# One list of parts per step in a relational graph layer: token values moved to GpSimd, degrees, statistics and normalisation cut into halves

## The chip, the cores and the metric

The kernel runs on one core of one Trainium2 chip. A core has five engines that work side by side, each through its own instructions in order: TensorE (PE, matrix products; its weight loads are shown as PEld), VectorE (DVE), ScalarE (ACT), GpSimd (POOL) and SyncE (SP, which here only issues DMAs). They wait for each other through semaphores. The metric is the device time of the whole program in microseconds (us), lower is better.

## The reference

One layer with a residual, over 64 samples of 256 tokens and 768 features, all in float32. `adj` holds integers 0 and 1 (about 1.6% ones) and is used both as adjacency and as relation index.

```python
h = jnp.maximum(_layernorm(x, axis=-1), 0.0)
adj = heads.astype(hs.dtype); radj = jnp.swapaxes(adj, 1, 2)
deg = adj.sum(-1); rdeg = radj.sum(-1)          # deg_c, rdeg_c: the same, 1 where 0
ctx = jnp.matmul(adj, hs @ Wadj.T + badj) / deg_c[..., None]
ctx = ctx + jnp.matmul(radj, hs @ Wrev.T + brev) / rdeg_c[..., None]
ctx = ctx + hs @ Wself.T + bself
agg = jnp.einsum('bij,bijr->bir', adj, E[rels])
rel = agg @ Wr.T + br * deg[..., None]
ragg = jnp.einsum('bij,bijr->bir', radj, E[rr])
rel = rel + ragg @ Wrr.T + brr * rdeg[..., None]
x = x + ctx + rel
```

## The kernel before

**What is multiplied.** The three 768x768 products of a sample are one product of a left matrix (256 tokens by three blocks: aggregated over `adj`, aggregated over its transpose, and the tokens themselves) with a right matrix (three weight blocks by three thirds of 256 output columns). The tokens are cut into halves a and b, so the left blocks are called a0, a1, a2, b0, b1, b2. Instead of 18 block products the kernel makes 15, each of a sum of left blocks with a sum of weight blocks (table `PRODUCTS`: number, left sum, right sum). GpSimd makes the left sums (`combine_left`, L490); the weight sums are made once.

**Two sweeps.** The weights of 15 products don't fit at once. Sweep 1 makes products 10, 5, 8, 11, 14, 2, 3, 13 for all 64 samples, keeps the left blocks in DRAM (`store_left`) and the partial output; sweep 2 loads both (`load_left`, `load_sums`) and makes products 7, 9, 15, 6, 4, 12, 1.

**Words.** From some sample on (`IN_WORDS`: product 9 or 7 from 1, 5, 15 and 4 from 2, 10 from 3, 11 from 4) a product is made from left and right values that were each split into a rounded part and a rest (`split_left`, `split_right`); its first two passes are `product_first` (L496), written "10a", "5a", "11a" below, and its third is in `product` (L507).

**A step of sweep 1** (`step1(t)`) does three samples at once: the products of M = t; for A = t+1 the aggregation (`aggregate`, six parts u0 to u5: four matmuls into a PSUM bank `pa`, L473, then a DVE product with the row of reciprocal degrees into `X`, L478), the token features (`self_features`, two GpSimd passes over `xT`, L462, then a Relu on ScalarE, L465) and the left sums; for N = t+2 the degrees (ScalarE sums over `adj`), the layer norm's statistics, and the normalised rows `hilo` in two words (ScalarE L424, DVE L430). `pa` has two PSUM banks, so the matmuls of part u(k+2) wait until DVE has read part u(k).

**Token values.** `statistics` (L373) makes mean and variance of N with the DVE's batch-norm instructions (L379, L380), and then a handful of tiny instructions on 2 to 20 numbers a partition: variance plus epsilon (L381), its power -0.5 on GpSimd (L382), the negated mean (L383), degrees clipped to 1 (L390), their reciprocal (L391), and a copy (L393). The tile `cols` then goes through a PE transpose (`pt`, L400), ScalarE (`line`, L402), DRAM (`d`, L405) and a broadcast load (`row`, L407). The next step's aggregation and `self_features` read `row`.

**The order.** The whole program is under manual scheduling: each engine runs its instructions in the order in which the Python code emits them. `ORDER1` and `ORDER2` list the products and, as plain numbers, the aggregation parts; `others_of_step`, `first_step`, `last_step` and `start` hang all other work on positions of that list. In `step1` the statistics of N are emitted at position 1, right behind part u0:

```python
if k == 0:
    degrees(N)
if k == 1:
    statistics(N)
```

A path for inputs with other integers in `adj` (`general_path`) follows and is skipped by a flag.

Of the kernel before, what the change touches and what calls it, by code (L numbers as in the profile page):

```python
# [9 lines left out]
F32 = mybir.dt.float32  # L10
# [7 lines left out]
P = 128  # L18
# [48 lines left out]


ORDER1 = (
    (10, "z", None, None),  # L70
    0,
    (5, "y", None, None),
    1,
    (10, "z", None, ((1, 1, 2),)),
    (5, "y", None, ((1, 1, 0),)),
    2,
    3,
    (8, "y", None, ((1, 1, 2),)),
    4,
    (11, "w", None, None),  # L80
    5,
    (14, "y", 2, ((-1, 0, 2),)),
    (11, "w", None, ((-1, 0, 2),)),
    (2, "z", 0, ((1, 0, 1),)),
    (3, "w", 1, ((1, 1, 2),)),
    (13, "y", 3, ((-1, 0, 0),)),
)
ORDER2 = (
    (7, "v", None, None),
    (9, "x", None, ((1, 0, 0),)),  # L90
    (15, "u", None, None),
    (7, "v", None, ((1, 0, 1, 2),)),
    (6, "x", None, ((1, 0, 1),)),
    (15, "u", None, ((1, 1, 1, 2),)),
    (4, "t", None, None),
    (12, "x", 4, ((-1, 1, 1),)),
    (4, "t", None, ((-1, 0, 1), (1, 1, 1))),
    (9, "x", None, None),
    (1, "x", 5, ((-1, 1, 0),)),
)  # L100
# [14 lines left out]
def kernel(  # L115
# [61 lines left out]
    others = const.tile([P, B], F32, name="others")  # L177
    flag = const.tile([1, 1], I32, name="flag")

    def main_path(main: ExitStack):  # L180
# [178 lines left out]
        def degrees(b):  # L359

            s = S[b]
            t = tok[b % 2]
            s["a"] = first2.tile([P, C, 2, L], F32R, tag="a", name=f"a_{b}")
            s["squares"] = first2.tile([P, C], F32, tag="squares", name=f"squares_{b}")
            for c in range(C):
                for k in range(2):
                    nc.scalar.activation(
                        s["a"][:, c, k, :], s["adj"][:, c, k, :], AF.Copy, accum_out=t[:, c, 4 - k : 5 - k]
                    )
                junk = first1.tile([P, L], BF16, tag="junk", name=f"junk_{b}_{c}")  # L370
                nc.scalar.activation(junk, s["adj"][:, c, 1, :], AF.Square, accum_out=s["squares"][:, c : c + 1])

        def statistics(b):  # L373
            s = S[b]
            t, v = tok[b % 2], cols[b % 2]
            stats = first2.tile([P, C, 2, 6], F32, tag="stats", name=f"stats_{b}")
            for c in range(C):
                for n in range(2):
                    nc.vector.bn_stats(stats[:, c, n, :], (s["o", c] if b == 0 else s["x"][:, c, :])[:, ts(n, HO)])  # L379
                nc.vector.bn_aggr(v[:, c, NMEAN : RSTD + 1], stats[:, c, :, :])  # L380
            nc.vector.tensor_scalar(v[:, :, RSTD], v[:, :, RSTD], EPS, None, op0=ALU.add)  # L381
            nc.gpsimd.tensor_tensor(v[:, :, RSTD], v[:, :, RSTD], half, op=ALU.pow)  # L382
            nc.vector.tensor_scalar(v[:, :, NMEAN], v[:, :, NMEAN], -1.0, None, op0=ALU.mult)  # L383

            rest = first2.tile([P, C], F32, tag="rest", name=f"rest_{b}")
            nc.vector.scalar_tensor_tensor(
                rest, s["squares"], 1.0, t[:, :, 3], op0=ALU.mult, op1=ALU.subtract, accum_out=others[:, b : b + 1]
            )
            nc.vector.tensor_scalar(t[:, :, 0:2], t[:, :, 3:5], 0.0, None, op0=ALU.is_gt)
            nc.vector.tensor_scalar(v[:, :, RDEG : RRDEG + 1], t[:, :, 3:5], 1.0, None, op0=ALU.max)  # L390
            nc.vector.reciprocal(v[:, :, RDEG : RRDEG + 1], v[:, :, RDEG : RRDEG + 1])  # L391
            to = v.rearrange("p c (k r) -> p c k r", k=2)[:, :, :, :NROW]
            nc.vector.tensor_copy(to, t.unsqueeze(2).to_broadcast([P, C, 2, NROW]))  # L393

        def spread(b):

# [518 lines left out]
```

## Time and profile before

| | |
|---|---|
| time, median of 2 runs | 3025.98 us (3023.38 and 3028.57) |
| the profiled execution's own time | 3028.58 us |
| its span, first to last instruction | 3026.8 us |
| mean granted TensorE clock | 0.971 of full |
| TensorE busy | 2797.6 us, 92% |
| VectorE / ScalarE / GpSimd busy | 2002.9 / 1495.4 / 1781.1 us |
| DMA moved | 698.50 MB, 231 GB/s on average |

What lies outside the span is 3028.58 - 3026.8 = 1.8 us. Sweep 1 takes the first two thirds of the span (TensorE's last product of sweep 1 ends at about 1942 us), sweep 2 the rest. A timeline row gives start, length, engine, line, operation, output and inputs, and in square brackets how long the engine stood idle before it and who ended that; when rows are pipelined, a row's length is a little more than the distance to the next. A row that begins with a stretch A:B gives for each engine its busy time there (with the number of instructions), then the granted clock, the share of time that the DMA engines were busy, and GB/s.

### The profile page before, as it was taken

What the parts mean: (1) busy time and instruction counts of PE and PEld (TensorE: products, weight loads), DVE (VectorE), ACT (ScalarE), POOL (GpSimd) and SP (SyncE); (2) the same over time, 40 slices, a digit from 0 to 9 for tenths busy, and PEclk for the clock granted to TensorE, in tenths of its full rate; (3) what the DMA queues carried; (4) which work ended last, traced back from release to release, by engine and by line L of the source; (5) the groups of instructions that cost most, each with busy time, mean ns of one, the idle gap of its engine ahead of it and who ended that gap; (6) DMA issues with size and microseconds to landing.
All of it is one profiled execution on the core that took longest, in us unless ns stands there. A gap on an engine that the chain in (4) does not pass through costs nothing.

```text
span 3026.8 us, 43782 instructions
## 1 busy us (share of the span) xinstructions
PE 2797.6 (92%) x16112; PEld 2516.0 (83%) x16112; DVE 2002.9 (66%) x3340; ACT 1495.4 (49%) x2734; POOL 1781.1 (59%) x905
## 2 busy tenths in 40 slices
PE   4779999999999999999999999799999999999999
PEld 2668888887887788888878888689999999999998
DVE  5466766766766767667667666466666666666665
ACT  3345555555555555555555555244444444444443
POOL 4365666666666656666666666555555555555553
PEclk8899999999999999999999999899999999999999
DMA  8456666666666666666666665667676667767674
GB/s 269 144 204 237 216 241 237 225 241 227 235 232 225 234 232 220 241 236 227 236 229 232 237 223 214 253 218 253 232 251 235 241 244 243 244 235 253 233 251 155
DMA packets 240355, 698.50 MB, mean 231 GB/s; under 512 B 19444, under 2 KB 100852, under 8 KB 223752
## 3 DMA queue, kind: packets, MB, share of 16 engines
q1 hardware_dynamic: 203272, 393.64, 39.5%
q10 hardware_dynamic: 36864, 302.01, 25.7%
q8 instruction: 129, 2.11, 0.3%
q14 instruction: 90, 0.74, 0.1%
HBM read 439.46 MB, written 256.11 MB: 230 GB/s over the span
## 4 chain that ended last, share of the span: by engine, by line
PE 58%; DVE 8%; issue 0%; DMA 0%; ACT 0%; POOL 0%; ACTq 0%; DVEq 0%; POOLq 0%
PE x L507 18%; PE y L507 9%; PE pa L473 4%; PE w L507 4%; PE u L496 3%; PE v L496 3%; PE t L496 3%; PE x L496 3%; PE z L507 3%; DVE cols L381 3%; DVE stats L379 2%; PE z L496 2%; PE u L507 2%; PE t L507 2%; PE w L496 2%; PE v L507 2%
## 5 line engine op out<-in xcount | busy, mean ns | idle before, releaser
L490 POOL TENSOR_TENSOR X<-X,Xs 128x768 f32<-128x768 f32 x256 | 473.3, 1861 | 497.4 <-DVE l L271 273.4
L473 PE MATMUL pa<-a,hilo 128*128 128x512 f32 x1536 | 437.8, 408 | 168.7 <-DVE X L478 144.9
L507 PE MATMUL y<-w,X 128*128 128x256 f32 x2304 | 578.8, 405 | 10.1 <-DVE o L520 6.4
L507 PEld LDWEIGHTS y<-w,X 128*128 128x128 f32 x2304 | 468.2, 205 | 88.4 <-issue 7.5
L473 PEld LDWEIGHTS pa<-a,hilo 128*128 128x128 f32 x1536 | 266.4, 192 | 238.2 <-DVE X L478 172.4
L462 POOL TENSOR_TENSOR xT<-xT,row 128x1536 f32<-128x1536 f32 (+1 forms) x128 | 447.7, 3498 | 16.3 <-DMA row<-d 11.3
L255 ACT ACTIVATE top<-l 128x768 f32<-128x768 f32 x350 | 285.4, 815 | 283.6 <-DVE l L272 174.0
L478 DVE TENSOR_TENSOR X<-pa,row 128x512 f32<-128x512 f32 x384 | 258.8, 687 | 186.6 <-PE pa L473 186.6
L507 PE MATMUL x<-w,X 128*128 128x256 f32 x1548 | 357.4, 381 | 7.9 <-DVE o L520 6.5
L272 DVE SCALAR_TENSOR_TENSOR l<-l,top 128x768 fp32r<-128x768 f32 x350 | 333.9, 954 | 12.1
L490 POOL TENSOR_TENSOR b2-a<-Xs,X 128x768 f32<-128x768 f32 x64 | 116.6, 1821 | 373.2 <-DVE X L478 373.2
L507 PEld LDWEIGHTS x<-w,X 128*128 128x128 f32 x1548 | 286.5, 191 | 42.5 <-issue 6.9
L490 POOL TENSOR_TENSOR a1+b<-X 128x768 f32<-128x768 f32 x64 | 117.1, 1829 | 268.2 <-PE w L507 246.6
L430 DVE SCALAR_TENSOR_TENSOR hilo<-x,cols,top_h 128x768 fp32r<-128x768 f32 x128 | 129.8, 1014 | 107.2 <-ACT top_h L255 107.1
L271 DVE TENSOR_TENSOR l<-X,top 128x768 fp32r<-128x768 f32 x186 | 176.8, 950 | 16.5 <-POOL X L490 16.5
L507 PE MATMUL w<-w,a1+b 128*128 128x256 f32 x768 | 178.6, 383 | 5.2 <-DVE o L522 5.2
L507 PE MATMUL x<-w,Xs 128*128 128x256 f32 x768 | 176.1, 379 | 0.0
L507 PE MATMUL z<-w,Xs 128*128 128x256 f32 x768 | 176.1, 379 | 0.0
L520 DVE TENSOR_TENSOR o<-o,x 128x256 f32<-128x256 f32 x128 | 53.9, 421 | 167.8 <-PE x L507 167.8
L507 PEld LDWEIGHTS w<-w,a1+b 128*128 128x128 f32 x768 | 143.2, 192 | 24.4 <-DVE o L522 5.8
L402 ACT ACTIVATE line<-pt 128x128 f32<-128x128 f32 x64 | 17.7, 277 | 293.4 <-PE pt L400 293.4
L465 ACT ACTIVATE Xs<-xT 128x1536 f32<-128x1536 f32 x64 | 95.0, 1484 | 127.2 <-POOL xT L462 123.2
(183 smaller groups left out, 5882.1 us busy)
## 6 DMA issues: line engine op xcount, KB each, us to landing
kept_X<-X ACTq DMA_DIRECT2D x64, 1536.0 KB
X<-kept_X ACTq DMA_DIRECT2D x64, 1536.0 KB
o<-in_x_dram SPq DMA_DIRECT2D x128, 384.0 KB
xT<-in_x_t_dram SPq DMA_DIRECT2D x64, 768.0 KB
kept_Xs<-Xs ACTq DMA_DIRECT2D x64, 768.0 KB
sums<-o SPq DMA_DIRECT2D x128, 384.0 KB
Xs<-kept_Xs ACTq DMA_DIRECT2D x64, 768.0 KB
o<-sums SPq DMA_DIRECT2D x128, 384.0 KB
```

Of the source, the lines that this page charges most:

```text
L255: nc.scalar.activation(top.rearrange("p (f i) -> p f i", i=of.shape[-1]), of, AF.Copy)
L271: nc.vector.tensor_tensor(others, value, top, op=ALU.subtract)
L272: nc.vector.scalar_tensor_tensor(diff, others.bitcast(F32), -STEP, top, op0=ALU.mult, op1=ALU.add)
L381: nc.vector.tensor_scalar(v[:, :, RSTD], v[:, :, RSTD], EPS, None, op0=ALU.add)
L430: nc.vector.scalar_tensor_tensor(hilo[:, 1, c, :], S[b]["x"][:, c, :], rstd, top, op0=ALU.mult, op1=ALU.subtract)
L462: eng.tensor_tensor(v, v, row[:, k : k + 1, :].to_broadcast([P, f1 - f0, L]), op=op)
L465: nc.scalar.activation(S[b]["Xs"], xT, AF.Relu)
L473: nc.tensor.matmul(pa, hilo[:, part, c, ts(f, P)], s["a"][:, c, :, :].rearrange("p s i -> p (s i)"), start=(k == 0), stop=(k == 2 * C - 1),)
L478: nc.vector.tensor_mul(s["X"][:, f, :, :].rearrange("p s i -> p (s i)"), pa, s["row"][:, 2:4, :].rearrange("p s i -> p (s i)"))
L490: (eng or nc.gpsimd).tensor_tensor(L[name], L[x], L[y], op=op)
L496: nc.tensor.matmul(bank, l[k][:, f, :], r[k][:, f, :], start=(k == 0 and f == 0), stop=(k == 1 and f == F - 1))
L507: nc.tensor.matmul(bank, l[:, f, :], r[:, f, :], start=(start and f == 0), stop=(row is None and f == F - 1), skip_group_check=not start,)
```

## The change

The two order tables and the functions around them are replaced by six strings. Each names the parts of a step in the order in which they are emitted; a mark ' behind a name means one sample later, '' two later. `FIRST` and `SECOND` are the first two steps with the start, `STEP1` a step of sweep 1, `LAST1` its last, `FIRST2` and `STEP2` sweep 2. `run` reads such a string and calls the functions. With it:

- `statistics`, `degrees`, `normalise` and `self_features` take a half (a token half, or one of the two passes), so that the halves are parts of their own at places of their own.
- The tiny instructions of `statistics` become `token_values`, a part of its own, and run on GpSimd, except the reciprocal, which stays on DVE. `others` has one number per token half and sample instead of one per sample.
- The products keep their operands. Their order in a step changes: 10a, 5a, 5, 10, 8, 11a, 11, 14, 3, 2, 13 with the aggregation in the order u1 u2 u0 u3 u4 u5; in sweep 2 the products' order stays.

```diff
-ORDER1 = (
-    (10, "z", None, None),
-    0,
-    (5, "y", None, None),
-    1,
...
+STEP1 = """
+left' degrees0'' u1' self0' 10a u2' 5a statistics0'' self1' u0' 5 statistics1'' 10 s11 degrees1'' adj''' o1' u3' relu' 8 11a u4' tokens'' u5' a0+a1+b0+b1 xt'' 11 normalise1'' b2-a1' spread'' store' second1'' a2+b2 14 b0+b1' s10' 3 normalise0'' second0'' a1+b1' 2 13 x''' out0 a1+b0+b1' out1 o0' s5'
+"""
...
+STEP2 = """
+7a a0+a2+b0+b2 a1+a2' b1+b2' a0+a2' 9 s4 15a 7 6 load'' s9' 15 4a tokT 12 s7' o0' 4 out0 s15' 9a' a0+a2+b2' 1 out1 o1'
+"""
...
-        def statistics(b):
+        def statistics(b, c):
+            s = S[b]
+            if c == 0:
+                s["stats"] = first2.tile([P, C, 2, 6], F32, tag="stats", name=f"stats_{b}")
+            for n in range(2):
+                nc.vector.bn_stats(s["stats"][:, c, n, :], (s["o", c] if b == 0 else s["x"][:, c, :])[:, ts(n, HO)])
+            nc.vector.bn_aggr(cols[b % 2][:, c, NMEAN : RSTD + 1], s["stats"][:, c, :, :])
+
+        def token_values(b):
+
             s = S[b]
             t, v = tok[b % 2], cols[b % 2]
...
-            nc.vector.tensor_scalar(v[:, :, RSTD], v[:, :, RSTD], EPS, None, op0=ALU.add)
+            nc.gpsimd.tensor_scalar(v[:, :, RSTD], v[:, :, RSTD], EPS, None, op0=ALU.add)
             nc.gpsimd.tensor_tensor(v[:, :, RSTD], v[:, :, RSTD], half, op=ALU.pow)
-            nc.vector.tensor_scalar(v[:, :, NMEAN], v[:, :, NMEAN], -1.0, None, op0=ALU.mult)
-
-            rest = first2.tile([P, C], F32, tag="rest", name=f"rest_{b}")
-            nc.vector.scalar_tensor_tensor(
-                rest, s["squares"], 1.0, t[:, :, 3], op0=ALU.mult, op1=ALU.subtract, accum_out=others[:, b : b + 1]
-            )
-            nc.vector.tensor_scalar(t[:, :, 0:2], t[:, :, 3:5], 0.0, None, op0=ALU.is_gt)
-            nc.vector.tensor_scalar(v[:, :, RDEG : RRDEG + 1], t[:, :, 3:5], 1.0, None, op0=ALU.max)
+            nc.gpsimd.tensor_scalar(v[:, :, NMEAN], v[:, :, NMEAN], -1.0, None, op0=ALU.mult)
+
+            nc.gpsimd.tensor_tensor(others[:, b, :], s["squares"], t[:, :, 3], op=ALU.subtract)
+            nc.gpsimd.tensor_scalar(t[:, :, 0:2], t[:, :, 3:5], 0.0, None, op0=ALU.is_gt)
+            nc.gpsimd.tensor_scalar(v[:, :, RDEG : RRDEG + 1], t[:, :, 3:5], 1.0, None, op0=ALU.max)
             nc.vector.reciprocal(v[:, :, RDEG : RRDEG + 1], v[:, :, RDEG : RRDEG + 1])
             to = v.rearrange("p c (k r) -> p c k r", k=2)[:, :, :, :NROW]
-            nc.vector.tensor_copy(to, t.unsqueeze(2).to_broadcast([P, C, 2, NROW]))
+            nc.gpsimd.tensor_copy(to, t.unsqueeze(2).to_broadcast([P, C, 2, NROW]))
...
-        def self_features(b, parts=((0, F),)):
+        def self_features(b, k):
...
+        def run(order, M, sweep, parts, places):
+
+            for item in order.split():
+                name = item.rstrip("'")
+                b = M + len(item) - len(name)
+                stem, digit = name[:-1], name[-1]
...
+                elif name in parts:
+                    part = parts[name]
+                    multiply(b, *part, sweep)
+                    if part[-1] and part[0] in IN_WORDS and b == IN_WORDS[part[0]] - 1:
+                        split_right(places, part[0])
+                elif name in of_sample:
+                    of_sample[name](b)
+                elif stem in of_part:
+                    of_part[stem](b, int(digit))
...
         for t in range(B):
-            step1(t)
+            order = FIRST if t == 0 else SECOND if t == 1 else STEP1 if t + 1 < B else LAST1
+            run(order, t, 1, PARTS1, PLACES1)
```

How the rows stand on VectorE in a steady step of sweep 1. In the names the first number after `pa` is the aggregation part, for `o` the token half, and after `X`, `y`, `z`, `l_11` the sample; the last is a running number; `waits` lists the semaphores. Before, products of sample 20:

```order
L478 TENSOR_TENSOR X_21_5030<-pa_0_5044,row_4898 128x512 [waits DMAHW7_49,DMAHW2_49,PE_49]
L380 BN_AGGR cols_104<-stats_5050 128x2 [waits DVE_49]
L381 TENSOR_SCALAR cols_104<-cols_104 128x2 [waits DVE_49]
L383 TENSOR_SCALAR cols_104<-cols_104 128x2
L386 SCALAR_TENSOR_TENSOR rest_5060,others<-squares_5035,tok_102 128x2 [waits Activation_49]
L389 TENSOR_SCALAR tok_102<-tok_102 128x2x2
L390 TENSOR_SCALAR cols_104<-tok_102 128x2x2
L391 RECIPROCAL cols_104<-cols_104 128x2x2 [waits DVE_49]
L393 COPY cols_104<-tok_102 128x4x5
L478 TENSOR_TENSOR X_21_5030<-pa_1_5080,row_4898 128x512 [waits PE_49]
```

The same engine after, products of sample 21:

```order
L401 BN_AGGR cols_105<-stats_5281 128x2 [waits DVE_49]
L543 TENSOR_TENSOR o_1_21_5083<-o_1_21_5083,z_21_5247 128x256 [waits PE_49]
L293 TENSOR_TENSOR l_11_21_5310<-X_21_4992,top_21_5313 128x768 [waits Activation_49]
L294 SCALAR_TENSOR_TENSOR l_11_21_5311<-l_11_21_5310,top_21_5313 128x768 [waits DVE_49]
L501 TENSOR_TENSOR X_22_5232<-pa_3_5325,row_5153 128x512 [waits PE_49]
L543 TENSOR_TENSOR o_1_21_5083<-o_1_21_5083,y_21_5267 128x256 [waits PE_49]
L501 TENSOR_TENSOR X_22_5232<-pa_4_5353,row_5153 128x512 [waits PE_49]
L414 RECIPROCAL cols_105<-cols_105 128x2x2 [waits Pool_49]
L501 TENSOR_TENSOR X_22_5232<-pa_5_5367,row_5153 128x512 [waits PE_49]
L545 TENSOR_TENSOR o_0_21_5222<-o_0_21_5222,w_21_5339 128x256 [waits DMAHW6_49,DMAHW4_49,PE_49]
```

Between the statistics and part u1 stood six tiny instructions; now only the reciprocal is left, and it stands between parts u4 and u5 and waits for GpSimd.

GpSimd in the same place, before:

```order
L490 TENSOR_TENSOR a1+b_20_5010<-X_20_4789 128x768 [waits PE_49]
L490 TENSOR_TENSOR X_20_4789<-a1+b_20_5010,X_20_4789 128x6x128 [waits DMAHW4_49,Pool_49]
L462 TENSOR_TENSOR xT<-xT,row_4898 128x1536 [waits DMAHW7_49,DMAHW2_49]
L462 TENSOR_TENSOR xT<-xT,row_4898 128x1536 [waits Pool_49]
L382 TENSOR_TENSOR cols_104<-cols_104,half 128x2 [waits DVE_49]
L490 TENSOR_TENSOR X_20_4789<-X_20_4789 128x6x128
```

and after:

```order
L513 TENSOR_TENSOR a1+b_21_5198<-X_21_4992 128x768 [waits PE_49]
L513 TENSOR_TENSOR X_21_4992<-a1+b_21_5198,X_21_4992 128x6x128 [waits DMAHW6_49,Pool_49]
L485 TENSOR_TENSOR xT<-xT,row_5153 128x1536 [waits DMAHW4_49,DMAHW0_49]
L485 TENSOR_TENSOR xT<-xT,row_5153 128x1536 [waits Pool_49]
L407 TENSOR_SCALAR cols_105<-cols_105 128x2 [waits DVE_49]
L408 TENSOR_TENSOR cols_105<-cols_105,half 128x2 [waits Pool_49]
L409 TENSOR_SCALAR cols_105<-cols_105 128x2
L411 TENSOR_TENSOR others<-squares_5235,tok_103 128x2 [waits Activation_49]
L412 TENSOR_SCALAR tok_103<-tok_103 128x2x2
L413 TENSOR_SCALAR cols_105<-tok_103 128x2x2
L416 COPY cols_105<-tok_103 128x4x5 [waits Pool_49]
L513 TENSOR_TENSOR X_21_4992<-X_21_4992 128x6x128
```

Six tiny instructions have joined the power behind the two passes over `xT`, ahead of the sum a0+a1+b0+b1 (last row) that product 14 reads. The copy (L416) doesn't wait for DVE's reciprocal.

More of the change, by code (lines that the diff above doesn't have):

```diff
@@ L357, in store_sums, with degrees @@
             nc.sync.dma_start(to[:, c, :], s["o", c])
-        def degrees(b):
+        def degrees(b, c):
             s = S[b]
             t = tok[b % 2]
[L363 to L371, printed above, removed]
```

333 lines of the change are left out of this document (111 added, 222 removed).

## The prediction

> **What bounds the kernel now.** I read the page's busy times first, then busy times by stretch, since two sweeps with a start and a seam can't be read from one average.
>
> ```profile
> span 3026.8 us, 43782 instructions
> PE 2797.6 (92%) x16112; PEld 2516.0 (83%) x16112; DVE 2002.9 (66%) x3340; ACT 1495.4 (49%) x2734; POOL 1781.1 (59%) x905
> ```
> ```profile
> 0.00:215.20 215.20, 139.77 (x552) 111.94 (x553) 116.21 (x190) 81.54 (x155) 98.13 (x53) 0.85 0.59 205
> 215.20:1880.40 1665.20, 1535.92 (x8296) 1351.15 (x8295) 1146.78 (x2092) 892.62 (x1742) 1073.59 (x523) 0.98 0.65 231
> 1880.40:2000.00 119.60, 100.61 (x507) 89.05 (x506) 65.01 (x78) 37.30 (x47) 62.49 (x30) 0.89 0.64 230
> 2000.00:3000.00 1000.00, 1000.00 (x6628) 944.16 (x6628) 664.26 (x965) 479.18 (x783) 546.84 (x301) 1.00 0.69 240
> ```
>
> The first number behind each length is PE. Sweep 2 (fourth row) has PE busy for 1000.00 of 1000 us at full clock: no order can gain there. What can be gained lies in the start (75 us idle), in steady sweep 1 (1665.20 - 1535.92 = 129 us idle, and a clock of 0.98), and in the seam (19 us). Steady sweep 1 is 58 steps, between the ends of product 13 of steps 3 and 61; the last row ends step 62.
>
> ```profile
> 214.90 0.47 PE L512 MATMUL y<-rows,tokT 128*128 128x256 f32 x1
> ...
> 1880.13 0.47 PE L512 MATMUL y<-rows,tokT 128*128 128x256 f32 x1
> ...
> 1905.51 0.47 PE L512 MATMUL y<-rows,tokT 128*128 128x256 f32 x1
> ```
>
> (1880.13 - 214.90) / 58 = 28.71 us a step. Step 62 has no sample N, so no statistics and no token values, but all products and all six aggregation parts: 1905.51 - 1880.13 = 25.38 us. The PE work of a step thus fits in 25.4 us plus one transpose, and 3.3 us a step are something else. The list of PE's waits and the timeline of one step name it:
>
> ```profile
> PE pa L473 <- DVE X L478: 144.9, 62, 7.0
> ```
> ```profile
> 1026.35 1.08 PE L473 MATMUL pa<-a,hilo 128*128 128x512 f32 x4
> 1029.65 1.19 PE L473 MATMUL pa<-a,hilo 128*128 128x512 f32 x4 [2.22 <-DVE X L478]
> 1030.68 2.75 PE L507 MATMUL y<-w,X 128*128 128x256 f32 x12
> ...
> 1057.65 1.27 PE L473 MATMUL pa<-a,hilo 128*128 128x512 f32 x4 [2.22 <-DVE X L478]
> 1058.71 4.42 PE L507 MATMUL y<-w,X 128*128 128x256 f32 x12
> ```
>
> Once a step PE stands 2.22 us, 62 times, for a bank that DVE hasn't read. Behind every second gap (this one, not the one before) twelve matmuls take 4.42 instead of 2.75 us: the clock has dropped. That is 1.67 us in two steps, 0.8 a step. 25.4 + 2.2 + 0.8 = 28.4 of the 28.7. Why is DVE late? Its timeline there, and GpSimd's:
>
> ```profile
> 1025.78 2.66 DVE L381 TENSOR_SCALAR cols<-cols 128x2 f32<-128x2 f32 x1
> 1028.35 0.15 DVE L383 TENSOR_SCALAR cols<-cols 128x2 f32<-128x2 f32 x1
> ...
> 1028.57 0.16 DVE L390 TENSOR_SCALAR cols<-tok 128x4 f32<-128x4 f32 x1
> 1028.76 0.18 DVE L391 RECIPROCAL cols<-cols 128x4 f32<-128x4 f32 x1
> 1028.86 0.15 DVE L393 COPY cols<-tok 128x20 f32<-128x20 f32 x1
> 1028.91 0.69 DVE L478 TENSOR_TENSOR X<-pa,row 128x512 f32<-128x512 f32 x1
> ```
> ```profile
> 1021.33 7.09 POOL L462 TENSOR_TENSOR xT<-xT,row 128x1536 f32<-128x1536 f32 x2
> 1028.52 0.70 POOL L382 TENSOR_TENSOR cols<-cols,half 128x2 f32<-128x2 f32 x1
> 1029.18 1.83 POOL L490 TENSOR_TENSOR X<-X 128x768 f32<-128x768 f32 x1
> ```
> ```profile
> L381 DVE TENSOR_SCALAR cols<-cols x64: 169/2655/2684, 6.8 to 1858.0; 128x2 f32<-128x2 f32 x64
> ```
>
> L381 works on two numbers a partition and takes 2655 ns (median) or 169 (least). It ends at 1028.44, when the two GpSimd passes over xT end (1028.42). It is stuck behind them, and with it, in DVE's order, the X that PE waits for. [...]
>
> **The change, part by part.** *Token values to GpSimd.* L381 leaves DVE, and the xT passes are ahead of the new instructions on GpSimd itself, so nothing on DVE stands behind them but the reciprocal, between u4 and u5. Gain: the gap, and the clock that drops behind it, if nothing else is late. What is late next?
>
> GpSimd gets six tiny instructions (the power was there). No row shows them on it; the nearest:
>
> ```profile
> L382 POOL TENSOR_TENSOR cols<-cols,half 128x2 f32<-128x2 f32 x64 | 44.8, 700 | 35.9 <-DVE cols L383 27.0 <-DVE cols L381 2.7
> ...
> masks.py:199 POOL TENSOR_SCALAR_AFFINE_SELECT ident<-ident 128x128 f32<-128x128 f32 x1 | 0.3, 292 | 0.1
> ...
> L904 POOL MEMSET const-float32-1.0<- 128x1 f32 x1 | 0.1, 98 | 0.0
> ```
>
> So 0.1 to 0.7 us each, 0.6 to 4.2 together; I take 1.5 (0.25 each), near the middle row, since add, compare and copy have no power in them. They can't be a gain on GpSimd. Product 14 waits for a0+a1+b0+b1, which stands behind them. GpSimd's chain to it begins where product 3 has read a1+b1 (its buffer is then free). These rows give its parts on PE and GpSimd:
>
> ```profile
> 1014.80 2.75 PE L507 MATMUL w<-w,a1+b 128*128 128x256 f32 x12
> ...
> 1017.51 2.75 PE L507 MATMUL y<-w,X 128*128 128x256 f32 x12
> ...
> 1025.63 0.88 PE L507 MATMUL y<-w,l 128*128 128x256 f32 x6
> ```
> ```profile
> 1045.63 1.82 POOL L490 TENSOR_TENSOR a1+b<-X 128x768 f32<-128x768 f32 x1 [4.32 <-PE w L507]
> 1047.53 1.83 POOL L490 TENSOR_TENSOR X<-a1+b,X 128x768 f32<-128x768 f32 x1
> ```
>
> A product with its row matmul takes PE 1017.51 - 1014.80 = 2.71 us, a pass of words 1026.35 - 1025.63 = 0.72, a part's `pa` at most 1.08 (1026.35 above). After the change four of them (14, 3, 2, 13) end a step, so 14 begins 25.4 - 4 x 2.71 = 14.6 us into it, and from the end of product 3 to the next 14 there are 2 x 2.71 + 14.6 = 20.0 us. GpSimd needs 1.82 + 1.83 + 7.09 (xT) + 0.70 (power) + 0.6 to 4.2 + 1.83 = 13.9 to 17.5. It has 2.5 us left at the worst. The same sum from the other gate: the second half of the statistics is on DVE behind u1, u2 and u0. PE's u1, 10a, u2, 5a, u0 are 3 x 1.08 + 4 x 0.72 = 6.1 us; with DVE's X (0.69) and some 1.7 for an output sum and that half, 8.5. 8.5 + 0.70 + 0.6 to 4.2 + 1.83 = 11.6 to 15.2 against 14.6. So 0 to 0.6 us is lost, and 0 at the value taken.
>
> *The reciprocal* waits for GpSimd's clipping, at 9.8 to 13.4 us by the same sum. It stands behind u4, whose matmuls end 12.8 us into the step (14 begins at 14.6; ahead of it are u5 with 1.08 and 11's third pass with 0.72) and whose X ends at 13.5: it comes after GpSimd anyway. Queued behind it are u5, the output sums and the normalisation; for its result waits `pt`. It ends at 13.7, `pt` is due at 14.5: 0.8 us spare. It could itself be stuck behind a GpSimd sum (1.83 us, then 1.0 of it on PE). In 64 rows it never was:
>
> ```profile
> L391 DVE RECIPROCAL cols<-cols x64: 178/178/180, 11.6 to 1861.0; 128x4 f32<-128x4 f32 x64
> ```
> That is with GpSimd in the power (1028.52 to 1029.22), not in a sum, so the bound stays: 0 to 1.0 us a step; I take 0, as GpSimd's sum will mostly have ended.
>
> [...]
>
> *Halves and order.* DVE is busy 1146.78 / 58 = 19.8 us a step, 2.5 of it L381's stall, so about 17 of 25.4 remain; ACT 15.4, GpSimd 18.5 + 1.5. None becomes the bound. The loads: SP issues `row` once `pt`'s line is written; GpSimd's next xT pass needs it.
>
> ```profile
> 1005.89 0.61 SPq L405 DMA_DIRECT2D d<-line  x2
> 1009.58 0.35 SPq L407 DMA_DIRECT2D row<-d  x1
> ```
> ```profile
> 14.36 0.35 SPq L407 DMA_DIRECT2D row<-d  x1
> ```
> ```profile
> 18.09 3.73 POOL L462 TENSOR_TENSOR xT<-xT,row 128x768 f32<-128x768 f32 x2 [8.06 <-DMA row<-d]
> ```
> Issue to use was 18.09 - 14.36 = 3.7 us at the start; in the steady step xT began 1021.33 - 1009.58 = 11.8 us after the issue without waiting. Now `d` goes out at 15.1 us, `row` 3.7 later (1009.58 - 1005.89) at 18.8, and xT's passes may start as late as 14.4 + 25.4 - 7.09 - 0.70 - 1.5 = 30.5: 11.7 us. Enough. The load of x, the stores and the second sweep's loads move in SP's and ACT's queues too; sweep 2's PE has no gap and the same products in the same order, so they cost 0 there; cover is GpSimd's lead of half a step. If it is gone, a late `load''` costs up to 2 us a step, 120 in all; nothing in the rows asks for that.
>
> *Start and seam.* In step 2 PE stands twice for DVE:
>
> ```profile
> 159.48 2.07 PE L473 MATMUL pa<-a,hilo 128*128 128x512 f32 x4 [6.98 <-DVE X L478]
> 166.30 5.25 PE L507 MATMUL y<-w,X 128*128 128x256 f32 x12 [4.74 <-DVE o L520]
> ```
> The second is an output sum of product 5 queued behind the splitting of a weight; it now stands ahead of it: 4.7 us, and 2.5 of slow clock behind it, go. A few more go with the product order (14 and 11 ahead of part u0 in step 0); against it the reciprocal waits for xT passes on GpSimd in steps 0 and 1. I take a gain of 10; bounds -10 (one xT pair more in the way) and +38 (half of the 75 us idle). The seam's gaps come from loads and sums that stay: 0, bounds +-8.
>
> **The sum.** Steady step after: 25.38 + 0.1 for the transpose + 0.15 for small waits = 25.6. 58 x (28.71 - 25.6) = 180. With the start 190: 3028.58 (the profiled execution: span 3026.8 and 1.8 around it) - 190 = 2838. The runs' median, 3025.98, is 2.6 below this execution, so I say 2838.
>
> **Rivals.** *A part of the gap comes back* (GpSimd's tiny instructions cost more than the power, or the reciprocal gets stuck): 1 us on PE before 14 or `pt`, perhaps with 0.8 of slow clock. For it: no row shows these costs. Against: the slack above. 58 x (3.1 - 1.0 to 1.8) = 75 to 122, plus 10: 2895 to 2945.
>
> [...]
>
> *No change*: what stood behind L381 (x's load, the normalisation) takes the whole gap: 28.7 a step, and the start within +-10: 3019 to 3039. Against it is step 62, which shows all of the PE work without a gap.
>
> *Slower*: `row` lands late. GpSimd runs in order, so xT's passes hold up the token values behind them, these the reciprocal, and this DVE and `pt`. Every us beyond 11.7 from issue to landing costs PE one. Equal to before at 11.7 + 3.1 = 14.8; at 17 us, 58 x 2.2 = 128 slower, less 10: 3146. For it: 6 instructions more stand in that chain, and DMA traffic must go from 231 to 231 x 28.7 / 25.6 = 259 GB/s. Against: 3.7 us at the start, 11.8 without any wait in the steady step, and 240 GB/s in sweep 2.
>
> **Chances.** Forecast 0.64 (its own range 2808 to 2890: start +38 and small waits 0 below, 0.9 us a step above); part comes back 0.22; no change 0.09; slower 0.05. The range 2808 to 2945 takes in the first two, less the tails. 2% of 3026 is 61 us, which stands here for what a measurement tells from no change. Faster 0.85, within 2% 0.10, slower 0.05.
>
> **What would show it.** Right: PE's idle before `pa` from DVE X falls from 144.9 to below 20 us; the steps are 25.4 to 25.8 us; the granted clock in steady sweep 1 is 1.00; the reciprocal stays near 0.18 us; sweep 2 takes what it took. Wrong: a new line of PE waiting for `pt`'s columns or for GpSimd's X at product 14 (rival one), SP or GpSimd waiting long for `row` (slower), or sweep 2 with PE gaps.

## The result, and the profile after

The changed kernel takes 2838.56 us (median of 2 runs, 2837.70 and 2839.43) against 3025.98 us: a ratio of 0.9381, 95% interval 0.9340 to 0.9421. The profiled execution took 2839.43 us, its span 2837.7. The prediction said 2838.

The page's busy times, and then busy times by stretch (PE first behind the length; the granted clock, the DMA share and GB/s are the last three columns): start, steady sweep 1, seam, steady sweep 2.

```profile
span 2837.7 us, 43467 instructions
PE 2736.3 (96%) x16112; PEld 2488.7 (88%) x16112; DVE 1817.8 (64%) x2892; ACT 1498.4 (53%) x2734; POOL 1864.6 (66%) x1289
```
```profile
0.00:205.00 205.00, 135.42 (x542) 107.86 (x543) 103.56 (x145) 78.64 (x152) 106.32 (x88) 0.88 0.59 207
205.00:1690.00 1485.00, 1482.00 (x8300) 1331.55 (x8299) 980.50 (x1687) 900.02 (x1745) 1143.92 (x871) 1.00 0.74 260
1690.00:1820.00 130.00, 106.72 (x572) 94.75 (x571) 70.84 (x86) 39.34 (x51) 69.63 (x31) 0.91 0.61 221
1820.00:2810.00 990.00, 990.00 (x6565) 934.14 (x6564) 651.98 (x957) 474.06 (x778) 544.22 (x300) 1.00 0.68 241
```

In steady sweep 1, PE is idle for 3 us of 1485 (before, 129 of 1665), at full clock instead of 0.98. DVE has lost 166 us of busy time there (1146.78 to 980.50): most of it was no work, but L381's stall (58 times 2655 - 169 ns, 144 us). The last matmul of product 13 in steps 3, 4 and 61 (its start is taken as the step's end, here as in the prediction):

```profile
206.90 0.47 PE L535 MATMUL y<-rows,tokT 128*128 128x256 f32 x1
...
235.94 0.47 PE L535 MATMUL y<-rows,tokT 128*128 128x256 f32 x1
...
1690.96 0.47 PE L535 MATMUL y<-rows,tokT 128*128 128x256 f32 x1
```

Steps 5 to 61 take (1690.96 - 235.94) / 57 = 25.53 us each, all within 0.01; step 4 takes 29.04 (DVE waits 3.28 us there for the load of x). Over the 58 steps of the prediction that is (1690.96 - 206.90) / 58 = 25.59 in place of 28.71: 181 us. Step 3 ends 214.90 - 206.90 = 8.0 us earlier. From the end of step 62 (1905.51 before, 1716.36 after) to the end of the span there are 1121.3 us in both kernels. 181 + 8 + 0 = 189 = 3026.8 - 2837.7.

The waits of PE that the argument needs (total, times, longest), and one step (it starts at 1002.05) on GpSimd and DVE:

```profile
PE y L530 <- ACT y L522: 9.5, 1, 9.5
PE y L530 <- POOL X L513: 9.2, 1, 9.2
PE pa L496 <- DVE X L501: 9.2, 4, 3.7
```
```profile
1001.22 7.08 POOL L485 TENSOR_TENSOR xT<-xT,row 128x1536 f32<-128x1536 f32 x2 [0.73 <-DMA row<-d]
1010.31 0.22 POOL L407 TENSOR_SCALAR cols<-cols 128x2 f32<-128x2 f32 x1 [2.01 <-DVE cols L401]
...
1012.28 1.85 POOL L513 TENSOR_TENSOR X<-X 128x768 f32<-128x768 f32 x1
1016.94 1.81 POOL L513 TENSOR_TENSOR b2-a<-Xs,X 128x768 f32<-128x768 f32 x1 [2.81 <-ACT hilo L446]
```
```profile
1015.19 0.69 DVE L501 TENSOR_TENSOR X<-pa,row 128x512 f32<-128x512 f32 x1 [1.91 <-PE pa L496]
1015.80 0.17 DVE L414 RECIPROCAL cols<-cols 128x4 f32<-128x4 f32 x1
1016.10 0.69 DVE L501 TENSOR_TENSOR X<-pa,row 128x512 f32<-128x512 f32 x1
```

The wait of 144.9 us in 62 pieces is down to 9.2 in 4, and nothing that comes once a step has taken its place (9.5 and 9.2 above it are single waits, at the seam and in step 0). a0+a1+b0+b1 ends at 1014.13 and product 14 starts at 1016.74: GpSimd has 2.6 us to spare. The reciprocal comes when GpSimd has long finished the values.

### The profile page after: what moved, and what is told of

The parts are those of the page before. It is cut to its first block, busy times and chain, and to the rows that moved or that the text cites. A ratio compares the mean times of both kernels' runs of the same rounds, so it can differ in the third digit from the quotient of the medians.

```text
span 2837.7 us, 43467 instructions
## 1 busy us (share of the span) xinstructions
PE 2736.3 (96%) x16112; PEld 2488.7 (88%) x16112; DVE 1817.8 (64%) x2892; ACT 1498.4 (53%) x2734; POOL 1864.6 (66%) x1289
## 4 chain that ended last, share of the span: by engine, by line
PE 93%; DVE 3%; DMA 2%; ACT 1%; issue 0%; POOL 0%; ACTq 0%; SPq 0%; DVEq 0%; POOLq 0%
PE y L530 19%; PE x L530 19%; PE pa L496 12%; PE z L530 7%; PE w L530 7%; PE u L519 3%; PE v L519 3%; PE t L519 3%; PE x L519 3%; PE w L519 3%; PE y L519 3%; PE z L519 3%; PE u L530 2%; PE v L530 2%; PE t L530 2%; DVE w L258 1%
## 5 line engine op out<-in xcount | busy, mean ns | idle before, releaser
L530 PE MATMUL y<-w,X 128*128 128x256 f32 x2304 | 536.4, 383 | 18.9 <-POOL X L513 9.2
L530 PEld LDWEIGHTS y<-w,X 128*128 128x128 f32 x2304 | 432.2, 192 | 80.1 <-POOL X L513 9.5
L496 PE MATMUL pa<-a,hilo 128*128 128x512 f32 x1536 | 416.1, 399 | 33.5 <-DVE hilo L452 18.2
L291 ACT ACTIVATE l<-X 128x768 fp32r<-128x768 f32 x186 | 155.6, 836 | 22.4 <-issue 19.9
L530 PEld LDWEIGHTS z<-w,Xs 128*128 128x128 f32 x768 | 142.7, 192 | 18.9
L530 PEld LDWEIGHTS x<-w,Xs 128*128 128x128 f32 x768 | 141.0, 190 | 17.1 <-DVE o L543 0.4
L545 DVE TENSOR_TENSOR o<-o,y 128x256 f32<-128x256 f32 x128 | 53.5, 418 | 156.7 <-PE y L535 156.7
```

What stands on the lines that cost most here:

```text
L291: nc.scalar.activation(first, value, AF.Copy, scale=LOWER)
L496: nc.tensor.matmul(pa, hilo[:, part, c, ts(f, P)], s["a"][:, c, :, :].rearrange("p s i -> p (s i)"), start=(k == 0), stop=(k == 2 * C - 1),)
L530: nc.tensor.matmul(bank, l[:, f, :], r[:, f, :], start=(start and f == 0), stop=(row is None and f == F - 1), skip_group_check=not start,)
L545: nc.vector.tensor_sub(o, o, bank)
```

## Experiments

The theory: once a step DVE was stuck ahead of an X that PE waits for, and what counts is what stands ahead of X in DVE's order and until when. But the change did several things at once: another engine, another place, halves, another order of products. Each run below takes these apart. "A step" is the mean of steps 4 to 61, from the ends of product 13 as above.

| run | us (median) | ratio to before, 95% | a step, us |
|---|---|---|---|
| before | 3025.98 | | 28.71 |
| after | 2838.56 | 0.9381 (0.9340 to 0.9421) | 25.59 |
| GpSimd, same place | 3187.98 | 1.0533 (1.0515 to 1.0550) | 31.39 |
| GpSimd, later | 2845.98 | 0.9399 (0.9383 to 0.9415) | 25.72 |
| DVE, later | 2843.71 | 0.9397 (0.9381 to 0.9413) | 25.69 |
| after, values on DVE | 2949.48 | 0.9750 (0.9734 to 0.9766) | 27.51 |
| after, values on DVE in two pieces | 2839.80 | 0.9382 (0.9366 to 0.9398) | 25.53 |
| after, tiny DVE operations put in | 2870.62 (one) | | 26.04 |
| after, one sum more | 2837.78 (one) | | 25.57 |
| after, two sums more | 2923.85 (one) | | 26.95 |
| after, other seam | 2845.70 | 0.9404 (0.9391 to 0.9417) | 25.58 |
| after, other seam and start | 2840.75 | 0.9388 (0.9375 to 0.9401) | 25.58 |
| the same, flag's sum mended | 2837.07 | 0.9371 (0.9358 to 0.9384) | 25.54 |
| DVE later, statistics later | 2920.02 | 0.9640 (0.9627 to 0.9653) | 27.02 |

### Only the engine: GpSimd, at the same place

```diff
-            nc.vector.tensor_scalar(v[:, :, RSTD], v[:, :, RSTD], EPS, None, op0=ALU.add)
+            nc.gpsimd.tensor_scalar(v[:, :, RSTD], v[:, :, RSTD], EPS, None, op0=ALU.add)
...
             nc.vector.reciprocal(v[:, :, RDEG : RRDEG + 1], v[:, :, RDEG : RRDEG + 1])
...
-            nc.vector.tensor_copy(to, t.unsqueeze(2).to_broadcast([P, C, 2, NROW]))
+            nc.gpsimd.tensor_copy(to, t.unsqueeze(2).to_broadcast([P, C, 2, NROW]))
```

> The kernel before, its order kept; only the token values go to GpSimd, at the place where they stood (behind the statistics, ahead of u1's X in DVE's order). Queue theory (what matters is what stands ahead of X in DVE's order, and until when): the reciprocal stays ahead of X and now waits for GpSimd's two xT passes and six small instructions behind them (1.8 us in the changed kernel from the first of them to the last), so X starts about 1.6 us later than before, PE's gap grows from 2.2 to about 3.8 us, and the clock may drop each time: 58 x (1.6 to 2.5) = 93 to 145 slower, 3119 to 3171 us. [...]

3187.98 us, 5.3% slower than before. DVE, then PE, of one step, and the wait:

```profile
1043.26 0.18 DVE L388 RECIPROCAL cols<-cols 128x4 f32<-128x4 f32 x1 [4.68 <-POOL cols L387]
1043.35 0.66 DVE L475 TENSOR_TENSOR X<-pa,row 128x512 f32<-128x512 f32 x1
```
```profile
1044.07 2.07 PE L470 MATMUL pa<-a,hilo 128*128 128x512 f32 x4 [3.81 <-DVE X L475]
1045.94 3.45 PE L504 MATMUL y<-w,X 128*128 128x256 f32 x12
```
```profile
PE pa L470 <- DVE X L475: 237.9, 63, 8.8
```

No operation on DVE is stuck any more, yet X is later: the reciprocal waits in its place for GpSimd's passes and values. PE's gap is 3.81 us instead of 2.22, and behind it the matmuls are slow. The sign and the gap came out as the queue theory has them; the loss was 159 us of span (3185.8 - 3026.8) where 145 was its upper end. The clock accounts for part of what is over: its mean over the 58 steady steps is 0.94, where it was 0.98 before. Moving the values to GpSimd, taken by itself, loses.

### Only the place: GpSimd later, and DVE later

```diff
+                if k == 6:
+                    token_values(N)
```

In both, `statistics` (at k == 1) is cut in two, and the token values are made behind part u2. In the first they are on GpSimd, in the second they stay on DVE.

> The kernel before with token values on GpSimd and emitted after part u2 of the step, when the xT passes end; nothing else of the order changed, no halves of degrees, statistics or normalisation. Queue theory: GpSimd's tokens end about 10.3 us into the step, pt is due at 11.0 and product 14 at 13.8, so nothing new is late: 25.6 to 25.9 us a step in place of 28.7, a gain of 160 to 180, 2845 to 2866 us. Rival (the whole new order, with its halves, is needed, else another wait takes the place of the first): 2950 us or more, with a new row of PE waits for pt's columns or for DVE's X.

> The kernel before with the token values still on DVE, but emitted after part u2 of the step; no instruction changes its engine. Queue theory: L381's operation (here the tensor_scalar with EPS) meets at most the last 0.9 us of the xT passes, and u1's X no longer stands behind it: 25.6 to 25.9 us a step, 2845 to 2866 us, with the operation at 0.2 to 1.0 us in place of 2.66. Rival (the engine matters, GpSimd has to take the values): the operation is stuck again and PE's wait for X stays, 2950 us or more.

2845.98 and 2843.71 us, at the lower end of what the queue theory had (2845 to 2866) and just below it. The group of the stuck instruction, in the second:

```profile
L385 DVE TENSOR_SCALAR cols<-cols 128x2 f32<-128x2 f32 x64 | 11.0, 172 | 0.1
```

172 ns on average in place of 2655: the same instruction on the same engine, two parts later. This alone gives 182 of the 187 us. Neither the engine nor the new list of parts is needed for the bulk of the gain. Most of their steps take 25.5 to 25.6 us, nearly as in the changed kernel, but about every sixth is slow (over 25.7), by up to 1.6 us. In one such step, on DVE:

```profile
1056.24 0.69 DVE L482 TENSOR_TENSOR X<-pa,row 128x512 f32<-128x512 f32 x1 [0.71 <-PE pa L477]
1058.17 1.02 DVE L379 BATCH_NORM_STATS2 stats<-x 128x6 f32<-128x384 f32 x2 [1.24 <-DMA x<-in_x_dram]
```

The statistics wait for the load of x, with the next X behind them. Here they are due 3.2 us into the step (1056.93 of a step that starts at 1053.70), in the changed kernel the first half starts at 4.1 and the second at 6.9; it has no slow step after the fourth. In the run with the values on DVE, eight of the ten slow steps behind the fourth have such a wait for x, of 0.57 to 1.28 us, and no other step has more than 0.28; the other two wait for an output sum. In the run on GpSimd the waits for x fit less well: one of 0.60 stands in a step that isn't slow, and three of its eight slow steps have less than 0.3.

### Statistics later, in one piece

The natural next step: the second of these runs, with the statistics one part later too, so that x is there.

```diff
-                if k == 1:
+                if k == 3:
                     statistics(N)
```

> The kernel before with the token values on DVE behind u2 (as in the run with that alone) and the statistics moved from behind u0 to behind u1, one part later in DVE's order; all else as before. That run's steps were 25.49 us, but about every seventh took up to 1 us more, and in the one looked at DVE waited 1.24 us for the load of x at the statistics, with u1's X behind them. If these waits are what the finer order of the changed kernel covers: the steps are 25.5 us throughout, about 10 us less than that run, 2828 to 2838 us. Rival (the slow steps come from something else, the row load or GpSimd): 2840 to 2846 us, with slow steps as before.

2920.02 us: the expectation was wrong by 80. Nearly every step takes 26.9 us now. PE's waits:

```profile
PE y L511 <- DVE o L524: 45.5, 61, 10.5
PE pt L404 <- POOL cols L386: 22.6, 58, 0.4
```
```profile
1051.20 0.41 DVE L524 TENSOR_TENSOR o<-o,y 128x256 f32<-128x256 f32 x1
```
```profile
1051.76 2.83 PE L511 MATMUL y<-w,X 128*128 128x256 f32 x12 [0.56 <-DVE o L524]
```

The four statistics and two aggregations are 2.4 us of DVE in one piece (1048.59 to 1050.97 in this step). At the new place the output sums of products 10 and 5 stand behind them, and product 8, which goes on in the bank of 5, waits for the second (0.56 us a step); the values end later too, and `pt` waits 0.39. The steps grow by more than the two waits together, 1.4 us. I had looked at what the statistics wait for and not at what stands behind them. This is what the halves can be good for: in the changed kernel the same work is two pieces of 1.3 us with an X and an output sum between them. That the load of x makes the slow steps is not shown by this run, since its longer steps give every load more time; for it speaks only that the waits for x and the slow steps mostly go together in the run before it.

### The order of the changed kernel, with the values on DVE

In one piece at the same place (behind u4's X), and then in two: the part that needs the mean and the variance right behind the statistics, the rest at the old place.

```diff
-            nc.gpsimd.tensor_scalar(v[:, :, RSTD], v[:, :, RSTD], EPS, None, op0=ALU.add)
+            nc.vector.tensor_scalar(v[:, :, RSTD], v[:, :, RSTD], EPS, None, op0=ALU.add)
...
-u0' 5 statistics1'' 10 s11
+u0' 5 statistics1'' rstd'' 10 s11
```

The last two lines are of the second run alone.

> The changed kernel, its order kept, with the token values back on DVE at the same place (behind u4's X, 13.5 us into the step), the power on GpSimd. Queue theory: nothing on DVE is stuck (GpSimd is idle then, each operation about 0.17 us), but GpSimd's power now waits for DVE until 13.7, and behind it in GpSimd's order a0+a1+b0+b1, which ends at about 16.3 where product 14 is due at 14.6: PE waits 1.6 to 2.0 us a step at product 14, perhaps with 0.8 us of slow clock: 58 x (1.6 to 2.8) = 93 to 162 slower than the changed kernel, 2931 to 3001 us. Rival (only the order of X against the values matters): 2838 us.

> The changed kernel with all its parts and its order, but the token values back on DVE in two pieces: EPS, the power (on GpSimd as ever) and the sign of the mean right behind the second half of the statistics, 8.4 us into the step, when the xT passes have ended (6.2); the values of the degrees at the old place behind u4. Queue theory: nothing on DVE is stuck and GpSimd never waits for DVE with a sum behind it: 25.4 to 25.6 us a step, 2830 to 2842 us, as the changed kernel (25.53 us a step, 2838.6). Rival (the values have to be on GpSimd for the new order to work): as in the run with the same order and the values on DVE in one piece, 27.45 us a step, 2949 us.

2949.48 us in one piece. Again nothing on DVE is stuck; the wait is on the other side:

```profile
PE y L533 <- POOL X L516: 95.0, 59, 11.2
```
```profile
1047.01 0.70 POOL L408 TENSOR_TENSOR cols<-cols,half 128x2 f32<-128x2 f32 x1 [8.50 <-DVE cols L409]
1047.68 1.81 POOL L516 TENSOR_TENSOR X<-X 128x768 f32<-128x768 f32 x1
```
```profile
1049.54 2.86 PE L533 MATMUL y<-w,X 128*128 128x256 f32 x12 [1.45 <-POOL X L516]
```

GpSimd stands 8.5 us at the power, waiting for DVE, with a0+a1+b0+b1 behind it, and product 14 is 1.45 us late. In two pieces (2839.80 us, steps of 25.53) both waits are gone, as the queue theory had it. So in this order the values may be on either engine, provided that what GpSimd needs from DVE comes before DVE's own late work. GpSimd is a good place for them there because its order holds no X.

### Which operations are stuck, and what it costs now

```diff
-... self0' 10a u2' 5a ...
+... self0' 10a u2' probe 5a ...
```

`probe` is one instruction on a small tile of its own, in six forms by turns.

> The changed kernel with one tiny extra DVE instruction a step behind u2's X, while GpSimd's second xT pass runs (2.7 to 6.2 us into the step): by the sample's number modulo six a tensor_scalar with a constant on 128x2 (the form of the old line L381), a reciprocal on 128x4, a copy of 128x20, a product of two 128x2 tiles, a scalar_tensor_tensor of two 128x2 tiles, a memset. If any DVE instruction is stuck behind the passes, all six rows show 2 to 3 us. [...] Each form that is stuck delays the statistics and u0's X behind it by 2 to 3 us in one step of six; if PE feels that, such a step takes 27 to 28.5 us in place of 25.53.

The groups by form (total, then the mean in ns):

```profile
L427 DVE COPY scr<-scr 128x20 f32<-128x20 f32 x11 | 27.1, 2463 | 0.0
L429 DVE TENSOR_TENSOR scr<-scr 128x2 f32<-128x2 f32 x10 | 24.9, 2491 | 0.0
L431 DVE SCALAR_TENSOR_TENSOR scr<-scr 128x2 f32<-128x2 f32 x10 | 23.1, 2310 | 0.0
L423 DVE TENSOR_SCALAR scr<-scr 128x2 f32<-128x2 f32 x10 | 21.6, 2159 | 0.0
L425 DVE RECIPROCAL scr<-scr 128x4 f32<-128x4 f32 x10 | 1.7, 168 | 0.0
L433 DVE MEMSET scr<- 128x2 f32 x10 | 0.6, 60 | 0.0
```

Four forms take 2.2 to 2.5 us on average: the copy, the product of two tiles, the `scalar_tensor_tensor` and the operation with a constant. Two take what they take elsewhere in the kernel: the reciprocal 168 ns (169 at L414), the memset 60 (60 at L198). So it is not any DVE instruction that is stuck next to the passes; what sets the four forms apart from the two is not shown by this run. The prediction had kept up to 1.0 us a step for a reciprocal stuck behind a sum of GpSimd; next to the passes over `xT` it isn't stuck (166 to 169 ns in ten steps).

The price is the second finding. By form, the steps with a reciprocal or a memset take 25.53 us on average, as without the probe, and those with one of the four stuck forms 26.20 to 26.43: 0.7 to 0.9 us for each stuck one. That is less than expected (27 to 28.5 for such a step). In the kernel before, a stall of the same length cost 3 us a step. By the two orders, u2 and u3 stood side by side there and u3 waited for the bank at once, while in the changed kernel passes of words stand between all the parts around the place; that this is the reason was not tried by itself.

### How much room GpSimd has

```diff
-u5' a0+a1+b0+b1 xt''
+u5' a0+a1+b0+b1 a0+a1+b0+b1 xt''
```

The same sum once more, and twice more in the second run.

> The changed kernel with a0+a1+b0+b1 summed twice on GpSimd in each of steps 2 to 62 (the result is the same), 1.85 us more in the chain that product 14 waits for. By the timeline of the changed kernel the sum ends 2.6 us before product 14: 25.53 us a step, no change (2838). If GpSimd's slack is not what the timeline shows (its later sums, or xT, are late then), 26 us a step or more.

> The same with the sum made three times, 3.7 us more: by the timeline product 14 is 1.1 us late each step: 26.6 to 27.1 us a step, 2902 to 2931 us, with a row of PE waits for POOL's X of about 60 x 1.1 = 66 us or more and no drop of the clock (gaps of 1.45 us in the run with the values on DVE in one piece had none). If 25.5, the slack is larger than the timeline says.

2837.78 us with one, 2923.85 with two:

```profile
1058.72 5.68 POOL L513 TENSOR_TENSOR X<-X 128x768 f32<-128x768 f32 x3
```
```profile
1064.45 2.86 PE L530 MATMUL y<-w,X 128*128 128x256 f32 x12 [1.12 <-POOL X L513]
```

1.85 us fit into the 2.6, 3.7 do not, and what is over (1.1) is PE's wait. The steps grow from 25.53 to 26.90, 0.25 more than the wait.

### Start and seam

What PE still loses is at the start and between the sweeps. Three runs move parts there and leave the steady steps as they are.

```diff
-10a sweep2 5a 10 5 V7 V9 V15 s11 V6 V4 V12 flag a0+a2^ ...
+10a 5a 10 sweep2 5 V7 V9 V15 s11 V6 V4 V12 a0+a1+b0+b1 a2+b2 8 V1 a0+a2^ ... 11 left1 ... 3 flag ...
```

> The changed kernel with another order between the sweeps only: in the last step of sweep 1 the second sweep's loads for sample 1 stand behind product 11 instead of ahead of product 5's second half (ACT's queue holds the scale of y behind their issue, and PE waits 9.54 us for it), a0+a1+b0+b1 and a2+b2 stand ahead of the second sweep's sums on GpSimd, and in the first step of sweep 2 product 6 stands ahead of 7, so that its output sum isn't behind the splitting of 7's weight (PE waits 7.95 us). If these waits are what the seam costs: 9.5 + 8.0 and some slow clock less, 2818 to 2828 us. Rival (the seam is bound by its loads, which fill the DMA engines from 1720 to 1765, so PE waits for a weight or a sum later instead): 2832 to 2840 us.

> The same, and another order of the first step: row's transpose and the normalisation of sample 1 ahead of the first products, the rows' preparation before the weight on which ACT waits 22 us, products 5 and 10 changed about, the weights' sums w2 and w3 ahead of sample 1's parts. If PE's waits of 9.19, 6.91 and 8.42 us there come from that order: step 0 ends at 75 to 90 instead of 99 us, and 5 to 20 us less than the run with the seam alone. Rival (the start is bound by loads, which fill the DMA engines from 30 to 60 us): within 4 us of it.

2845.70 and 2840.75 us, no gain; the first was expected at 2818 to 2828 and the second 5 to 20 below the first. The two waits at the seam that were aimed at went, but `flag`, moved behind the weights' sums, made a worse one in both (17.8 in the first, 17.6 in the second):

```profile
PE pf L571 <- DVE total L569: 17.8, 1, 17.8
```

At the start, step 0 ends at 95.16 us, not at 75 to 90: two of the three waits aimed at there went and the third shrank (8.42 to 2.23), but PE now waits 8.08 us for ACT and twice 5.06 for DVE, each time for a weight that they prepare. That fits the rival (the start is bound by loads), though its sign of being right, within 4 us, was missed too (4.95).

The third run makes the flag's sum ahead of product 8 (and moves the weights' sums and splittings behind output sums).

> The run with start and seam, with the sum of flags made ahead of product 8 and its matmul behind 11's first half (there PE waited 17.6 us for it, behind weights' sums on DVE that waited for their loads), the sums v6, v4 and v1 moved behind product 13's and 9's output sums, and the splitting of the weights 9 and 7 behind the output sums of 6 and 12. Theory: the 17.6 us were one wait; without it sweep 1 ends 17 us earlier, the loads (DMA engines full until 1765 us) then give part of it back: 10 to 18 us less than that run, 2822 to 2831 us. Rival (sweep 2 can't start before its weights have landed, so any wait taken away at the seam comes back there): 2834 to 2842 us.

2837.07 us (ratio 0.9371, 0.9358 to 0.9384): no difference from the changed kernel that can be told. Step 63 now takes 21.0 us instead of 36.1, and all of it comes back (from the end of step 62 to the end of the span 1123.9 us, 1121.3 in the changed kernel). The three longest waits of PE behind step 63 (a fourth, of 2.23 us, is for a weight's load), and the two stretches there:

```profile
1749.88 4.74 PE L530 MATMUL x<-w,Xs 128*128 128x256 f32 x12 [6.43 <-DVE w L258]
...
1762.88 4.40 PE L530 MATMUL x<-w,X 128*128 128x256 f32 x12 [3.08 <-DVE o L543]
...
1770.89 1.65 PE L519 MATMUL x<-w,l 128*128 128x256 f32 x6 [3.40 <-ACT l L291]
```
```profile
1735.33:1764.00 28.67, 16.93 (x68) 13.82 (x67) 9.68 (x8) 3.06 (x3) 10.57 (x6) 0.88 0.96 336
1764.00:1782.00 18.00, 13.80 (x44) 10.90 (x44) 14.50 (x14) 7.77 (x8) 9.01 (x5) 0.62 0.14 45
```

Until 1764 the DMA engines are full (0.96), then DVE is (14.50 of 18 us), with the splitting of weights and left values. The time is the one of the rival (2834 to 2842). That the loads bound the seam, and DVE behind them, is read from the trace and wasn't tried by itself. None of the three versions beats the changed kernel by more than can be measured.

## Why the prediction was right

**The bound.** The stall ahead of X and the slow clock behind it were 3.1 us a step, and both went: 181 us of steady gain against 180. (The clock's part, 0.8 from "every second gap", was 0.7: it dropped in 24 of 58 steps.) The floor taken from step 62 (25.38, and a transpose) was the right one: the steps are 25.53. Of the 0.15 us for small waits, 0.05 are there in 57 steps; step 4, 3.5 us longer, adds 0.06 a step on average. That the forecast and the median agree to 1 us is luck in part: 190 us less than the median of 3025.98 would have been 2836, and 2838 was worked out from the profiled execution, which came out at 2839.43.

**Token values on GpSimd.** Six small instructions were taken at 1.5 us from rows of 0.1 to 0.7 us. Two of their groups (total, mean in ns, then idle time before):

```profile
L409 POOL TENSOR_SCALAR cols<-cols 128x2 f32<-128x2 f32 x64 | 15.9, 249 | 4.3
L412 POOL TENSOR_SCALAR tok<-tok 128x4 f32<-128x4 f32 x64 | 14.8, 231 | 0.0
```

All six lie between 202 and 249 ns and make 1.34 us. The statistics were put at 8.5 us into the step (8.2), the end of a0+a1+b0+b1 with the values taken at 12.5 (12.1), product 14 at 14.6 (14.7), the reciprocal's end at 13.7 (13.9), `pt` at 14.5 (14.6). The room in front of product 14 is measured twice, by the timeline and by the added sums. That is why the first rival, a part of the gap that comes back, did not happen; the run with the values on DVE in the same order shows what it would have looked like (PE waits for the sum of product 14), at 2949.48 where the rival had 2895 to 2945.

**The reason.** It holds, but it is narrower than the prediction told it. I wrote the gain down to L381's leaving DVE. The runs show that leaving DVE is neither enough (3187.98 at the same place) nor needed (2843.71 on DVE, later). What gains is that the values no longer stand between the statistics and the next X. The prediction did have the piece for this ("nothing on DVE stands behind them but the reciprocal, between u4 and u5"), and never said that the reciprocal's place carries the whole of it.

**The start.** 8.0 us against 10, but not by the parts that I named. Step 0, which was to gain by products 14 and 11 ahead of u0, ends 6.0 us later (99.12 for 93.11): product 14 waits 9.2 us for its sum on GpSimd, which stands behind the rows' preparation. Steps 1 to 3 make up 14.0, above all step 2 (35.54 for 46.60), where the two waits that I quoted were. The size was right by two errors that cancel, which is luck.

**The seam and sweep 2.** 0 and 0, as said. The load queues moved without harm: `row` is issued 18.95 us into the step and GpSimd's pass starts 5.5 us later, and the prediction gave it 11.7.

```profile
1021.00 0.35 SPq L430 DMA_DIRECT2D row<-d  x1
```
```profile
POOL xT L485 <- DMA row<-d: 65.9, 62, 4.3
1026.51 3.49 POOL L485 TENSOR_TENSOR xT<-xT,row 128x1536 f32<-128x1536 f32 x1 [0.49 <-DMA row<-d]
```

GpSimd now waits for `row` about 1 us in every step, where the prediction counted on none; it costs nothing, since GpSimd then waits 2.0 us for the statistics anyway. The 11.7 were too much. They let GpSimd's values end just ahead of `pt`, but behind them in its order stands a0+a1+b0+b1 (1.83), which product 14 needs: 14.6 - 1.83 in place of 14.4 gives 10.1. The trace agrees: 5.5, the 2.0 that GpSimd waits for the statistics, and the 2.6 that it has ahead of product 14 make 10.1. So 4.6 us were to spare, and the rival with a late `row` was nearer than the prediction had it.

**The range.** Its lower end was 2808, but its own terms (28 us more at the start, 0.15 us less in 58 steps) add up to 2801; the result lies far from both.

**No change** as a rival needed something behind L381 to take the whole gap; step 62 had spoken against it, and rightly.

## What to carry to other kernels

Where one engine waits for another every step, look at what stands ahead of the awaited instruction in that engine's order and what that stands waiting for; moving it past the awaited instruction may give all of the gain, and moving it to another engine at the same place can lose more than there was to win. Before a piece of work is moved, list what comes to stand behind it: 2.4 us of statistics one part later cost 1.4 us a step, through an output sum and through `pt`. A wait that is taken away where loads fill the DMA engines may come back at the next thing that needs them, as the 15 us of step 63 did here.

## What was not expected of the hardware

Gaps of PE and what followed: after 0.56, 1.12 and 1.45 us, in nearly every step of a run, twelve matmuls took 2.83 to 2.86 us, nearly as after none (2.75); after 1.92 us, once a kernel, 2.86 in the changed kernel and the first two runs on the seam, 4.24 in the run with tiny operations put in and 4.54 in the one with the flag's sum mended; after 2.22 us up to 4.44, as the clock dropped in 24 of the 58 steady steps of the kernel before; after 2.48 us, once, 4.51; after 3.81 us four matmuls of a part took 2.07 and the twelve 3.45, and the mean clock over the 58 steady steps of that run was 0.94. So gaps of about 2 us cost the clock in some places here and not in others.

What differs between a gap of 2.22 us that drops it and the next that doesn't can be read from the granted clock. In the traces of the kernels before and after, all of its 71 and 17 changes lie on the edges of a fixed grid of windows of 3.41 us. Here are the windows around the two gaps that the prediction shows (PE's busy time stands behind the length, the clock third from the end):

```profile
1024.53:1027.95 3.42, 2.90 (x19) 2.30 (x17) 3.35 (x5) 1.93 (x4) 3.34 (x2) 1.00 0.43 159
1027.95:1031.36 3.41, 1.71 (x8) 1.46 (x9) 3.34 (x13) 1.49 (x1) 3.31 (x4) 1.00 0.85 284
1031.36:1034.77 3.41, 3.41 (x19) 2.95 (x18) 2.62 (x5) 0.59 (x2) 1.44 (x1) 1.00 0.65 216
...
1055.25:1058.67 3.42, 1.20 (x5) 0.86 (x5) 3.38 (x12) 1.48 (x1) 3.31 (x3) 1.00 0.51 159
1058.67:1062.08 3.41, 3.41 (x9) 2.66 (x8) 2.60 (x4) 0.00 (x0) 2.12 (x2) 0.50 0.97 339
```

The first gap is shared by two windows, which are busy for 2.90 and 1.71 us, and the clock stays. The second lies in one window, which is busy for 1.20 us, and the next window runs at 0.50 of the clock. In these two traces, every window at full clock (from 30 us on, but for the last 10 us) with PE busy for less than 0.40 of it was followed by half the clock (28 of 28 before, 8 of 8 after), none with more than 0.50 (0 of 780 and 0 of 787), and 7 of the 14 between before, 0 of 1 after. So what goes with the drop here is not the gap alone, but how much of one window stands idle: by these counts between 1.7 and 2.0 us of the 3.41, an estimate, as PE's busy time is modelled. It fits that a gap of 1.45 us left the twelve matmuls behind it at 2.86 us in all 57 steps that have it. No run tried this by itself.

A small instruction on GpSimd costs little: in the changed kernel 0.20 to 0.25 us for 2 to 20 numbers a partition, 1.3 to 1.6 times the 0.15 to 0.17 of the same work on DVE (148 to 158 ns at L383 to L393 before, 172 at L385 with the values on DVE later), and the power 0.74.
